# A pipelined two-layer window-attention and scan kernel: first loads moved ahead of the Toeplitz transfers, and own step tables for the first and the last rounds

## Chip, cores and metric

The kernel runs on one core of a Trainium2 chip. The metric is the device time of one execution in microseconds (us); the median of several runs is compared.

## The reference, cut to what matters

The input x has 32 images of 56 x 56 pixels with 96 channels. Two layers follow each other, each with a mixer and a feed-forward part, both added to their input.

```
x = x + attention(ln(x))     # 7x7 windows, 3 heads, rolled by 3 rows and columns
x = x + ffn0(ln(x))          # 96 -> 384 -> 96, fp8 products, fp16 sums, relu
x = x + scan(ln(x))          # expand and gate 96 -> 192, a linear recurrence along the
                             # 56 columns, times sigmoid(gate), 192 -> 96
x = x + ffn1(ln(x))          # as ffn0, with other weights
```

Within a row of 56 columns the recurrence is linear with fixed coefficients, so it is a product with a lower triangular Toeplitz matrix of 56 x 56 for each of the 192 channels. The kernel computes the 56 taps of each channel once, and then these matrices.

## The kernel before, in words

**Tiles.** An image is cut into 4 blocks of 14 rows, 128 blocks in all (`nblocks`). A block is one tile `xb` of 112 partitions by 7 by 96 floats, from a pool of 11 buffers; it is loaded in 6 DMAs (9 for the last block of an image, whose rows wrap round), worked on in place, and stored in as many. All loads and stores are issued by SyncE (SP), line 500 and line 506.

**Steps.** The work on a block is cut into 104 named steps, mostly one engine each. A name is a kind and a place. `s`, `p`, `n`, `t` are the four parts of a layer norm (`layer_norm`): statistics on VectorE (L442, L444), the power -1/2 on GpSimd (L450), the normalisation in seven instructions on VectorE (L460), the transpose on TensorE (L473, L475); the letter behind says which norm: `a` attention, `f` first feed-forward, `e` scan, `g` second feed-forward. `ea`, `ef`, `eg`, `xe` copy the transposed tile out of PSUM on ScalarE. Attention has `q`, `k`, `v`, `sc` (scores, L568), `st0` to `st2` (scores plus bias on VectorE, L599), `ex0` to `ex2` (exponential on ScalarE, L612), `av` (L650), `rc`, `tro`, `eo`, `pr` (L698), `ad` (add to xb, L492). A feed-forward part has `h`, `x`, `r`, `c` for three thirds (TensorE L718, ScalarE L730, VectorE L736, and the cast to fp8 at L742, on GpSimd for the second third and VectorE for the others), then `y` (TensorE L752), `z` (ScalarE L764), `b` (VectorE L770), `k` (GpSimd, add to xb, L774); so `hg2` is the first product of the third third of the second one. The scan has `r0` (GpSimd L795), `pu0` to `pu3` (L806, L807), `th` and `uc` (ScalarE L814, L819), and once in four blocks `SC0` to `SC5` (the Toeplitz products, L830) and `GA0` to `GA5` (gating on VectorE, L845); then `gt0`, `gt1` (transposes, L863), `eg0`, `eg1` (ScalarE L873), `so` (L884) and `as` (add to xb, L492). `LD` and `ST` are load and store.

**PSUM.** `banks` hands out four buffers of two banks each, in turn, to all steps that write PSUM; a step waits until the buffer of four steps earlier has been read.

**Order.** A table, `PIPELINED`, lists the steps as `name:lag`. The program is written out in rounds t = 0, 1, 2, ...; in a round each step of the table is issued, in the table's order, for block t - lag, if there is such a block. Lags go from 0 (`LD`) to 11 (`ST`, `zg`, `bg`, `kg`). So in the first rounds only the steps of small lag have a block, and in the last ones only those of large lag. Before the rounds are through, `add_manual_dep` fixes the order on each engine as written. Each engine works through its instructions in this order, and SP through its DMAs. A second table, `IN_TURN`, is for weights outside a bound; its branch isn't taken here.

**Toeplitz matrices.** VectorE makes the taps during the set-up. `load_toep`, called at the start of round 1, writes them repeatedly to a DRAM tile `taps_d` (one DMA of 4.7 MB, L266) and reads that back at skewed addresses in 18 DMAs (L274) into the two `gts` buffers, which later hold gates. `turn_toep`, at the start of round 5 (the smallest lag of a `th` step, since `th` is the first to write gates), copies them with two dimensions exchanged into `toep`, two copies on VectorE and two on ScalarE (L287).

Of the kernel before, what the change touches and what calls it, by code (L numbers as in the profile page):

```python
# [55 lines left out]
PIPELINED = (  # L56
# [7 lines left out]
)  # L64

IN_TURN = (
# [10 lines left out]
def kernel(  # L77
# [29 lines left out]
    nblocks = nimg * NBLK  # L107
# [32 lines left out]
    def zeros(size, name):  # L140
# [20 lines left out]
        fill=1.0,  # L161
# [71 lines left out]
    n = 1  # L233
# [29 lines left out]
    def load_toep():  # L263


        nc.sync.dma_start(taps_d.rearrange("w j e -> j w e"), taps_t[:, None, :].to_broadcast([2 * HW, HW, E]))  # L266
        src = taps_d[:, :, :]
        for half in (0, RS):

            for w0, w1 in ((0, 48), (48, HW - SH), (HW - SH, HW)):  # L270
                for t0, t1 in ((0, NRP), (NRP, HW - SH), (HW - SH, HW)):
                    w_in, w_out = (w0 + SH) % HW, (t0 + SH) % HW
                    first = w_in * 2 * HW + HW - w_in + w_out
                    nc.sync.dma_start(  # L274
                        gts[t0 // NRP][half + w0 : half + w1, t0 % NRP : t0 % NRP + t1 - t0].rearrange("w t e -> w (t e)"),
                        bass.AP(
                            tensor=src.tensor,
                            offset=src.offset + first * E,
                            ap=[[(2 * HW - 1) * E, w1 - w0], [1, (t1 - t0) * E]],
                        ),  # L280
                    )

    def turn_toep():
        toep3 = toep[:, 0 : E * HW].rearrange("p (e t) -> p e t", t=HW)
        for e0 in range(0, E, EH):
            for n, copy in enumerate((nc.vector.tensor_copy, nc.scalar.copy)):
                copy(  # L287
                    toep3[:, e0 : e0 + EH, n * NRP : (n + 1) * NRP],
                    gts[n][:, :, e0 : e0 + EH].rearrange("p t e -> p e t"),
                )  # L290
# [47 lines left out]
    def fill_bias(one):  # L338
        for b in bias:
            nc.vector.tensor_copy(b, one[:, None, :].to_broadcast([128, NPAIR, W2]))  # L340
        part = bias[1][:, NPAIR // 2 :, :]
        nc.vector.tensor_tensor(part, part, mask[:, None, :].to_broadcast([128, NPAIR // 2, W2]), ALU.add)
# [44 lines left out]
    for n in range(2):  # L387
# [10 lines left out]
        v = const.tile([128, NPAIR * NH, HD + 1], F32, name=f"v_{n}")  # L398
# [16 lines left out]
    step = {}  # L415
# [473 lines left out]
    feed_forward("g", 1)  # L889


    def pipeline(table):
        entries = [(n, int(lag)) for n, lag in (e.split(":") for e in table.split())]
        gates = min(lag for n, lag in entries if n[0:2] == "th")
        for t in range(nblocks + 1 + max(lag for _, lag in entries)):
            if t == min(1, gates):
                load_toep()
            if t == gates:
                turn_toep()
            for name, lag in entries:  # L900
                i = t - lag
                if name[0:2] in ("SC", "GA"):
                    if i % NBLK == 0 and 0 <= i < nblocks:
                        step[name](i // NBLK)
                elif 0 <= i < nblocks:
                    step[name](i)
        order = mybir.DependencyInfo(mybir.DependencyClass.NoSync, mybir.DependencyReason.DATA)
        last = {}
        for ins in nc.cur_bb.bb.instructions:
            if ins.engine in last:  # L910
                tc.add_manual_dep(ins, last[ins.engine], order, reason="order of the steps")
            last[ins.engine] = ins.name

    safe = nc.values_load(flag[0:1, 0:1], min_val=0, max_val=1)
    with tc.If(safe > 0) as branch:
        fill_bias(b1T)
        pipeline(PIPELINED)
    with branch.Else():
        fill_bias(b1)
        pipeline(IN_TURN)  # L920
# [49 lines left out]
```

## Time and profile before

| | |
|---|---|
| median of 3 runs | 3900.87 us (3891.35 to 3901.78) |
| the profiled execution | 3897.57 us, its span 3895.8 us |
| TensorE matmul busy | 3710.0 us, 95% of the span |
| VectorE busy | 3246.4 us, 83% |
| ScalarE busy | 2330.3 us, 60% |
| GpSimd busy | 1453.0 us, 37% |
| mean granted TensorE clock | 0.982 |
| bytes moved by DMA | 99.34 MB, 25 GB/s over the span |

The profile is one execution; its stretches are measured in microseconds from the start of the span. Busy time of TensorE (PE) counts matmuls, and PEld the loads of weights beside them. The granted clock is the share of TensorE's full clock that it was allowed in a stretch; the same matmul takes longer at a lower one. In the view of waits, a line names the waiting engine and line, what ended the wait, the total, how many times, and the longest.

Where the rounds stand in the span: the scores of block 0 (round 2) end at 44.24, the product `av` of block 0 (round 3) starts at 92.88, that of block 1 (round 4) at 113.56, the first copy of `turn_toep` (round 5) at 135.92, the first step of round 6 on TensorE at about 166.6 and of round 7 at 186.6. Round 130 starts at about 3737.6.

### The profile page before, as it was taken

The numbers are of one execution on the slowest core, as the hardware profiler recorded it, in microseconds if no ns is written. First come the engines' busy times: TensorE is split into PE (matmuls) and PEld (weight loads), VectorE is DVE, ScalarE is ACT, GpSimd is POOL, SyncE is SP. The second block draws the span as 40 slices with busy tenths as digits, with TensorE's granted clock in tenths as the row PEclk, the third lists the DMA queues.
The fourth block names the chain that finished last, engine by engine and source line by source line (L and its number), as shares of the span: only waits on it lengthen the run. The fifth ranks groups of instructions, "written<-read, shape, count | busy, mean of one in ns | idle before, by whom it ended". The sixth has DMA issues, their size and how long they took to land.

```text
span 3895.8 us, 178068 instructions
## 1 busy us (share of the span) xinstructions
PE 3710.0 (95%) x78628; PEld 3132.4 (80%) x78628; DVE 3246.4 (83%) x9420; ACT 2330.3 (60%) x4611; POOL 1453.0 (37%) x1176
## 2 busy tenths in 40 slices
PE   1899999999999999999999999999999999999996
PEld 1678888888888888888888888888888888888884
DVE  3678888888888888888888888888888888888864
ACT  0556666666666666666665666666666666656652
POOL 1333334333334343334433334433333433333432
PEclk7899999999999999999999999999999999999997
DMA  6000101001101011001110011110010100100100
GB/s 128 19 3 22 28 22 28 22 22 25 25 22 28 22 25 25 22 22 28 23 26 22 22 24 25 25 25 22 22 28 22 28 22 22 27 22 22 24 15 21
DMA packets 226267, 99.34 MB, mean 25 GB/s; under 512 B 218396, under 2 KB 225150, under 8 KB 225262
## 3 DMA queue, kind: packets, MB, share of 16 engines
q1 hardware_dynamic: 222522, 86.81, 9.9%
q8 instruction: 620, 10.16, 1.1%
q10 hardware_dynamic: 2964, 1.05, 0.1%
q14 instruction: 161, 1.32, 0.1%
HBM read 44.45 MB, written 43.35 MB: 23 GB/s over the span
## 4 chain that ended last, share of the span: by engine, by line
PE 89%; DVE 6%; DMA 2%; issue 1%; ACT 0%; POOL 0%; SPq 0%; ACTq 0%; DVEq 0%; POOLq 0%
PE pu L806 12%; PE scan L830 10%; PE so L884 9%; PE qk L526 7%; PE av L650 5%; PE gt L863 5%; PE pv L545 5%; PE pr L698 5%; PE pu L807 4%; PE s L568 4%; DVE pT L599 4%; PE py_g L752 4%; PE ph_g L718 4%; PE py_f L752 4%; PE tr_o L679 3%; PE ph_f L718 3%
## 5 line engine op out<-in xcount | busy, mean ns | idle before, releaser
L806 PE MATMUL pu<-weg,xs 128*128 128x288 f32 x1792 | 622.4, 429 | 0.7 <-issue 0.7
L730 ACT CAST h_g<-ph_g 128x784 f16<-128x784 f32 x384 | 300.3, 821 | 348.0 <-issue 330.4
L460 DVE TENSOR_SCALAR xn_g<-xb,st_g,rs_g 112x96 fp8e5<-112x96 f32 x896 | 365.8, 476 | 88.7 <-POOL rs_g L450 87.7
L830 PEld LDWEIGHTS scan<-u,toep 64*64 64x64 f32 x24576 | 386.4, 135 | 65.2 <-issue 42.9
L830 PE MATMUL scan<-u,toep 64*64 64x28 f32 x24576 | 413.8, 221 | 20.3 <-issue 18.9
L807 PEld LDWEIGHTS pu<-weg,xs 128*128 128x128 f32 x1792 | 341.4, 191 | 97.7 <-POOL xs L795 1.8
L819 ACT COPY u<-pu 128x384 f32<-128x384 f32 (+1 forms) x512 | 229.4, 448 | 298.3 <-PE pu L807 240.0
L742 POOL CAST hq_g<-h_g 128x784 fp8e5<-128x784 f16 x128 | 122.9, 960 | 751.6 <-DVE h_g L736 474.0
L450 POOL TENSOR_TENSOR rs_a<-rs_a,neg_half 112x7 f32<-112x7 f32 x128 | 190.8, 1490 | 560.1 <-DVE rs_a L444 560.1
L884 PEld LDWEIGHTS so<-wso,gT 128*112 128x112 f32 x3584 | 371.7, 179 | 9.1 <-PE ph_g L718 0.7
L884 PE MATMUL so<-wso,gT 128*112 128x96 f32 x3584 | 376.4, 263 | 0.0
L814 ACT ACTIVATE gt<-pu 128x384 f32<-128x384 f32 (+1 forms) x512 | 237.9, 465 | 212.2 <-PE pu L807 212.2
L845 DVE SCALAR_TENSOR_TENSOR gt<-gt,scan 128x448 f32<-128x448 f32 x384 | 220.5, 616 | 153.0 <-PE scan L830 152.9
L807 PE MATMUL pu<-weg,xs 128*128 128x96 f32 x1792 | 322.3, 262 | 2.6 <-issue 2.6
L526 PE MATMUL qk<-xw,wqkv 128*32 128x196 f32 (+1 forms) x3072 | 310.1, 394 | 2.6 <-ACT xw L516 2.3
L730 ACT CAST h_f<-ph_f 128x784 f16<-128x784 f32 x384 | 309.8, 807 | 1.7 <-DVE hq_g L742 0.9
L774 POOL TENSOR_TENSOR xb<-xb,y_f 112x672 f32<-112x672 f32 x128 | 187.3, 1463 | 292.4 <-DVE y_f L770 292.4
L806 PEld LDWEIGHTS pu<-weg,xs 128*128 128x128 f32 x1792 | 277.6, 192 | 18.9 <-issue 3.5
L650 PE MATMUL av<-v,pT 64*64 64x33 f32 x12288 | 212.7, 223 | 61.5 <-ACT pT L612 59.1
L718 PEld LDWEIGHTS <-w1q 128*128 128x128 fp8e5 x1536 | 123.0, 100 | 173.1 <-issue 79.2
L650 PEld LDWEIGHTS av<-v,pT 64*64 64x64 f32 x12288 | 196.9, 136 | 75.0 <-ACT pT L612 59.8
L599 DVE SCALAR_TENSOR_TENSOR pT<-s,bias 128x392 f32<-128x392 f32 (+1 forms) x512 | 213.6, 459 | 49.6 <-PE s L568 45.2
(147 smaller groups left out, 8653.0 us busy)
## 6 DMA issues: line engine op xcount, KB each, us to landing
xb<-in_x_dram SPq DMA_DIRECT2D x224, 126.0 KB
out_dram<-xb SPq DMA_DIRECT2D x224, 126.0 KB
taps_d<-u SPq DMA_DIRECT2D x1, 4704.0 KB
xb<-in_x_dram SPq DMA_DIRECT2D x224, 13.1 KB
xb<-in_x_dram SPq DMA_DIRECT2D x224, 7.9 KB
out_dram<-xb SPq DMA_DIRECT2D x224, 13.1 KB
out_dram<-xb SPq DMA_DIRECT2D x224, 7.9 KB
xb<-in_x_dram SPq DMA_DIRECT2D x32, 72.0 KB
```

What stands on the lines that cost most here:

```text
L460: nc.vector.tensor_scalar(xn[:, g, :], xb[:, g, :], mean[:, col], rs[:, col], op0=ALU.subtract, op1=ALU.mult, **saturate)
L526: nc.tensor.matmul(pq[j * rows : (j + 1) * rows, m, 0:size], wqkv[:, m * C + h0 * HD : m * C + h1 * HD], xws[i % 2][:, j * size : (j + 1) ...
L599: nc.vector.scalar_tensor_tensor(view(dst), src, QSCALE, view(bt), op0=ALU.mult, op1=ALU.add)
L650: nc.tensor.matmul(po[r * 64 : r * 64 + 64, k, n0 : n0 + HD + 1], pT[kp, h, pair * W2 : pair * W2 + 64], v[kp, pair * NH + h, :], start=Tr ...
L718: nc.tensor.matmul(ph[:, half, 0:HALF], w1q[:, hc * 128 : (hc + 1) * 128], xqs[layer][:, half * HALF : (half + 1) * HALF], start=True, sto ...
L730: nc.scalar.copy(h16.rearrange("p (h t) -> p h t", h=2), held.pop(("ph", n, i, hc))[:, :, 0:HALF])
L752: nc.tensor.matmul(po[:, g - g0, :], hq[hc][:, g * TP : (g + 1) * TP], w2q[:, hc, :], start=(hc == 0), stop=(hc == 2),)
L806: nc.tensor.matmul(pu[:, g, 0 : E + EH], rows[:, 0:128], weg[:, 0 : E + EH], start=True, stop=True)
L807: nc.tensor.matmul(pu[:, g, E + EH : 2 * E], rows[:, RS:], weg[:, E + EH :], start=True, stop=True)
L814: nc.scalar.activation(gt[:, rp : rp + n, :], held["pu", i, j][:, 0:n, 0:E], AF.Tanh, scale=0.5)
L830: nc.tensor.matmul(py[o0 : o0 + RS, eh, e * NRP : (e + 1) * NRP], toep[p * RS : (p + 1) * RS, ch * HW : ch * HW + RS], u[p * RS : (p + 1) ...
L884: nc.tensor.matmul(po[:, g - g0, :], gT[:, g - g0, eh, :], wso[:, eh, :], start=(eh == 0), stop=(eh == 1))
```

## The change

Three things are changed in `pipeline`, and two tables are added.

1. The loads of blocks 0 to 3 (`PRELOADED = 4`) are issued ahead of all rounds, and `load_toep` straight behind them, also ahead of the rounds. In the rounds `LD` issues only blocks from 4 on. `turn_toep` stays at the start of round 5.
2. Rounds 0 to 6 (`FILL_ROUNDS = 7`) follow a table `FILL`.
3. Rounds from 130 on (`nblocks + DRAIN_FROM`, 128 + 2) follow a table `DRAIN`. Rounds 7 to 129 follow `PIPELINED` as before.

Both tables hold the same 104 steps with the same lags as `PIPELINED`, in another order. In the branch of `IN_TURN` no other tables are given.

```diff
+FILL_ROUNDS = 7
+FILL = (
+    "gt0:9 hf0:4 r0:5 SC1:8 gt1:9 pu0:5 xf0:4 pg:10 ex2:3 hg1:10 SC2:8 ex0:3 pu1:5 eg:10 GA0:9 rf2:4 "
+    "cf1:4 pu2:5 xg1:10 th1:5 uc0:5 th2:5 SC5:9 rg1:10 ng:10 uc1:5 th0:5 ST:11 cg0:10 rg0:10 uc2:5 "
+    "cf2:4 sa:1 rf0:4 av:3 cf0:4 eg0:9 so:9 SC0:9 rc:3 kg:11 sg:9 GA2:9 zg:11 GA5:9 GA3:8 yf:4 zf:4 "
+    "tro:3 as:9 cg2:10 bf:4 kf:4 se:4 pa:1 ta:2 xg2:10 eo:3 GA1:8 rg2:10 ea:2 pe:4 pr:3 q:2 k:2 ad:3 "
+    "ek:2 bg:11 LD:0 yg:10 tg:10 pu3:5 uc3:5 cg1:10 sf:3 GA4:8 eq:2 th3:5 v:2 ne:4 ev:2 te:4 pf:3 "
+    "sc:2 xe:4 nf:3 tf:3 st1:2 ef:3 st0:2 st2:2 ex1:2 hf1:3 eg1:9 xf1:3 hg2:10 xg0:10 na:1 SC4:8 "
+    "hg0:10 hf2:3 xf2:3 SC3:8 rf1:3 "
+)
+DRAIN_FROM = 2
+DRAIN = (
+    "hf0:4 rf2:4 cf2:4 r0:5 SC5:9 xf0:4 LD:0 pu3:5 v:2 zg:11 pu2:5 uc3:5 eq:2 bg:11 st0:2 rf0:4 pg:10 "
+    "pu1:5 ex0:3 GA2:9 sa:1 cf1:4 th3:5 q:2 cf0:4 GA5:9 ng:10 th2:5 kg:11 ex2:3 uc2:5 yf:4 uc1:5 na:1 "
+    "SC0:9 GA0:9 st1:2 sc:2 th1:5 av:3 gt0:9 rc:3 zf:4 st2:2 bf:4 ea:2 tro:3 eo:3 eg0:9 ek:2 tg:10 "
+    "pr:3 pu0:5 eg:10 ad:3 gt1:9 hg2:10 sf:3 uc0:5 kf:4 se:4 eg1:9 pf:3 xg2:10 th0:5 SC4:8 nf:3 "
+    "hg0:10 tf:3 hg1:10 ta:2 rg2:10 xg1:10 pe:4 cg2:10 SC3:8 rg1:10 ef:3 pa:1 ne:4 xg0:10 GA4:8 "
+    "cg1:10 GA3:8 rg0:10 so:9 cg0:10 as:9 ev:2 hf1:3 hf2:3 SC2:8 ST:11 ex1:2 te:4 xf2:3 yg:10 xf1:3 "
+    "SC1:8 xe:4 GA1:8 sg:9 rf1:3 k:2 "
 )
...
-    def pipeline(table):
-        entries = [(n, int(lag)) for n, lag in (e.split(":") for e in table.split())]
-        gates = min(lag for n, lag in entries if n[0:2] == "th")
-        for t in range(nblocks + 1 + max(lag for _, lag in entries)):
-            if t == min(1, gates):
-                load_toep()
+    PRELOADED = 4
+
+    def pipeline(table, fill=None, drain=None):
+        tables = []
+        for text in (fill or table, table, drain or table):
+            tables.append([(n, int(lag)) for n, lag in (e.split(":") for e in text.split())])
+        gates = min(lag for n, lag in tables[0] if n[0:2] == "th")
+        for i in range(min(PRELOADED, nblocks)):
+            step["LD"](i)
+        load_toep()
+        for t in range(nblocks + 1 + max(lag for _, lag in tables[0])):
             if t == gates:
                 turn_toep()
-            for name, lag in entries:
+            for name, lag in tables[0 if t < FILL_ROUNDS else 2 if t >= nblocks + DRAIN_FROM else 1]:
                 i = t - lag
                 if name[0:2] in ("SC", "GA"):
                     if i % NBLK == 0 and 0 <= i < nblocks:
                         step[name](i // NBLK)
+                elif name == "LD":
+                    if PRELOADED <= i < nblocks:
+                        step[name](i)
                 elif 0 <= i < nblocks:
                     step[name](i)
...
-        pipeline(PIPELINED)
+        pipeline(PIPELINED, FILL, DRAIN)
```

More of the change, by code (lines that the diff above doesn't have):

```diff
@@ L63 @@
     "yg:10 sg:9 na:1 LD:0 rf1:3 "
+)
+FILL_ROUNDS = 7
+FILL = (
[7 rows of a table added]
+)
+DRAIN_FROM = 2
+DRAIN = (
[7 rows of a table added]
 )
```

## The prediction

> **What bounds the kernel now.** I read the 40 slices first, then busy time by stretch, the waits, and the chain of waits at both ends.
>
> ```profile
> span 3895.8 us, 178068 instructions
> ...
> PE   1899999999999999999999999999999999999996
> ...
> PEclk7899999999999999999999999999999999999997
> ```
>
> TensorE is at nine tenths in all slices but the first two and the last. Between the two ends it is the bound, and reordering the ends can't touch that. So I cut each end at its rounds (columns: stretch, length, busy us and instructions of PE, PEld, DVE, ACT, POOL, then granted clock, DMA share, GB/s).
>
> ```profile
> 89.30:113.56 24.26, 17.25 (x290) 12.99 (x290) 14.25 (x48) 9.15 (x18) 4.44 (x3) 0.70 0.47 108
> 113.56:135.92 22.36, 21.21 (x323) 17.29 (x324) 16.37 (x52) 8.58 (x17) 7.37 (x6) 0.69 0.01 2
> 135.92:166.60 30.68, 21.50 (x338) 17.51 (x337) 18.26 (x45) 20.62 (x27) 11.75 (x5) 0.78 0.01 2
> 166.60:186.60 20.00, 19.79 (x346) 15.41 (x347) 16.23 (x51) 12.94 (x28) 7.31 (x6) 1.00 0.01 2
> ```
>
> These are the end of round 2 with round 3, then rounds 4, 5 and 6. Round 6 is full (19.79 of 20.00). Round 5 is long because the turn of the Toeplitz matrices holds ScalarE for two copies (136.51 to 146.1). Before all that stands a hole, which the waits and the chain explain:
>
> ```profile
> DVE st_a L442 <- DMA xb<-in_x_dram: 55.4, 1, 55.4
> ```
>
> ```profile
> SPq L274 <- DMA gt<-taps_d: 28.1, 8, 7.1
> SPq L274 <- DMA taps_d<-u: 18.5, 1, 18.5
> SPq L266 <- DVE u L256: 10.7, 1, 10.7
> ```
>
> ```profile
> 22.97 18.87 DMA taps_d<-u
> ...
> 44.71 24.50 DMA gt<-taps_d
> 69.23 16.96 DMA gt<-taps_d
> 86.21 2.81 DMA xb<-in_x_dram
> ```
>
> VectorE waits once, for 55.4 us, for block 1. Its six loads stand on SP's queue behind the write of taps_d (from 22.97) and 18 reads of it; SP stops for each wait, so the loads are only issued from 78.64 to 86.2, and land at 89.0. Nothing else is missing then: the scores of block 0 ended at 44.24.
>
> The drain, by rounds 130, 131, 132, 133, 134, 135, 136, and 137 with the end:
>
> ```profile
> 3737.60:3760.60 23.00, 21.18 (x264) 17.83 (x264) 18.11 (x56) 15.88 (x33) 10.43 (x9) 0.97 0.06 15
> 3760.60:3780.10 19.50, 17.18 (x134) 14.20 (x133) 13.41 (x36) 10.57 (x21) 9.26 (x8) 0.85 0.07 16
> 3780.10:3799.30 19.20, 18.74 (x471) 16.44 (x472) 7.30 (x17) 7.62 (x16) 2.29 (x2) 0.92 0.08 18
> 3799.30:3826.70 27.40, 20.23 (x481) 17.11 (x481) 15.28 (x36) 6.31 (x10) 4.89 (x4) 0.81 0.06 14
> 3826.70:3841.70 15.00, 10.23 (x81) 8.01 (x80) 8.40 (x22) 5.50 (x9) 3.88 (x3) 0.87 0.10 22
> 3841.70:3857.40 15.70, 12.12 (x81) 9.69 (x79) 8.00 (x20) 5.50 (x9) 3.95 (x3) 0.69 0.08 19
> 3857.40:3874.40 17.00, 10.45 (x80) 8.07 (x77) 9.18 (x24) 6.28 (x11) 5.59 (x5) 0.83 0.09 19
> 3874.40:3895.80 21.40, 6.65 (x34) 3.94 (x34) 6.04 (x13) 3.89 (x7) 3.60 (x3) 0.50 0.15 33
> ```
>
> No engine is full from round 133 on: a chain from engine to engine sets the length, and part of PE's busy time is a halved clock (so takes 3.9 us at a low clock and 2.9 at a full one).
>
> [...] the 24 qk matmuls took 4.35 us at 36.7 and 2.34 us at 124.4 (the record of the granted clock says full speed in both[...]). [...] here xn_g takes 2.90 us for seven beside the xb add of GpSimd and 1.77 without it, in the drain too, and no order given by the tables parts them.
>
> **Part 1, loads in front.** Nothing is removed or added: 27 DMAs of blocks 0 to 3 (6, 6, 6 and 9) are issued before the taps_d write; 21 of them move past 19 transfers. Block 0's six took 2.42 us from 9.73 (0.40 each), so all end at 9.73 + 27 x 0.40 = 20.6. SP sat idle there anyway, in the 10.7 us that it waits for VectorE's taps, to 22.97. So the Toeplitz transfers start as before; the cover is 2.3 us wide, and if loads run slower, the excess delays the turn one for one. Their 1.2 MB should have landed by about 24 (2.8 us after the last issue, as at 86.2). I take 0 to 3 us of delay, value 0.5. Block 4's load now stands where block 1's did and lands at 89; it is first wanted in round 5 after the turn, so it costs nothing.
>
> Without the hole: sa of block 1 runs at 34 beside PE's work, and the score sums (st, 90.57 before) start when the scores end, at 44.35. From 90.57 to the turn's first copy (135.92) is 45.35 us, so with the old order the turn is reached at 44.35 + 45.35 = 89.7. The turn waits for the reads too. The last large one ended at 86.2; the small ones behind it I put at 87.5 (86.2 to 89). Behind the waiting turn stand, on VectorE, rf2, cf1 and sa of block 4, on ScalarE xf0 and ex2, and for these waits PE with av of block 2, once hf0 and three pu are through. So arrival and transfers come within 2 us of each other: **the stall that goes is succeeded at once by the Toeplitz transfers**, and no order of rounds 2 to 4 brings more than 135.9 - 86.2 = 49.7.
>
> **Part 2, the table for rounds 0 to 6.** Each step keeps its lag, so only the order on the engines changes. In rounds 3 and 4 sc comes before nf and tf, and the sums st follow nf, not sc: in round 4 before, VectorE ended xn_e at 131.76 and st began at 132.08, then xn_a and the turn; some 1.7 us of it overlap now. Against it, xf0 (0.81) stands before ex2 and ex0. Arrival 87 to 90; with the transfers' 87.5 + 0.5 the turn begins at about 88.5, so **47.4 us** come out (43 to 50). Round 5: pu2 now runs while ScalarE turns (1.4 us at full clock, 2.7 as at 149.7), xf0 costs 0.8 behind it: 1 us gained. The change of order at round 7 may cost as much (0 to 2, unseen in the trace). Fill: **47 us**, 42 to 52. From round 7 to 129 the order is the same and PE is full, so the shift stays.
>
> **Part 3, the table from round 130.** Rounds 134 to 136: the path runs as - cg0, rg1, rg2, cg2 - st_g - rs_g - xn_g - tr_g - gt1 - ph_g - so - as. Between as and st_g lie 0.47 + 0.68 + 1.09 = 2.24 us of VectorE casts; the new order puts sg straight behind as, and the casts beside so. In return hg2 (0.5) goes ahead of so, and xg0, rg0, cg0 end 0.3 after so does at best[...]. Net 2.2 a round by three rounds: 6.6. The last block has the same casts taken out before its st_g and none of the losses count in full: 2.2. Round 132/133: from so of block 123 (ends 3796.9) to that of 124 (3822.5) are 25.6 us, with 4.5 us of PE standing still between scans and about 2 of low clock; PE's work in it at full clock is 15.5, VectorE's chain (as, GA1, sg, GA2, GA5, ng, GA0) some 10 and gt, eg, so behind it 7. I take 19.6: 6.0. Round 131: before, ne (1.77) stands ahead of as, both h_g steps and cg2, and py_g waits for these until 3778; rg2, cg2 and rg1 now go ahead of it: 3. Round 130 has only 2 us in which PE isn't busy: 1. Sum 18.8; the change of order at 130 I charge 0.8 (0 to 3). **Drain 18 us**; low end 4 (only the casts, and half of them), high end 26.
>
> Behind the last add (ends 3887.9) nine stores and their landing take 8 us as before.
>
> **Sum.** 47 + 18 = 65. The profiled execution took 3897.57 (span 3895.8): 3832.6. The median of the three runs is 3.3 above it, so I take 3834 for a median.
>
> **Rivals.** (a) The forecast, 3834: 0.60. (b) The drain stays bound by the same chain, since its casts only move to stand ahead of as: fill 47, drain 4: 3850 (0.17). For it: py_g and xg0 need those casts in every round; against it: so takes 2.8 us or more, in which VectorE idles 2.1 to 3.2 us now. (c) The transfers take over in the fill: loads and reads collide, or the reads run slower beside a working core; turn at 95, fill 40, drain 16: 3845 (0.10). Against it: the loads fit into SP's idle time. (d) More in both, 52 + 26: 3823 (0.08). (e) **Slower**: an order handed over at round 7 with loads and stores at another phase makes each of the 123 steady rounds longer (28.87 us each: 186.6 to 3737.6). Saving is gone at 65 / 123 = 0.53 us a round, and it is slower by 0.3% at 0.62; at 0.75 it gives 3927. Against it: after 89 us no load was waited for again (one wait of 55.4 in all). 0.03. That the loads don't go ahead at all is excluded by block 0's, issued in its written place at 9.73; with the tables alone it would be near 3880 (0.02, with the same).
>
> **Range.** What a measurement can tell from no change here is about 0.3%, 12 us. (a), (b) and (c) reach from fill 52 and drain 26 to fill 42 and drain 4, with some 4 us between runs: 3815 to 3857. Left out are (e), the tables alone and half of (d). Faster 0.95, same 0.02, slower 0.03.
>
> **What would show it.** No st_a wait over 5 us; 27 xb loads on SP before 22.97; the turn's first copy at 87 to 90, released by gt or just behind it; PE busy from 45 to 88 with gaps in place of a hole; first hf0 of round 6 near 118; st_g straight behind as from round 133; so to so about 13 us in rounds 134 to 136. I am wrong if taps_d starts after 26, if a wait for gt holds the turn past 93, or if rounds 10 to 129 differ by more than 0.05 us each.

## The result, and the profile after

| | before | changed |
|---|---|---|
| median, four runs each on one chip | 3896.11 us (3883.43 to 3901.78) | 3844.48 us (3839.45 to 3848.43) |
| ratio, 95% interval | | 0.9871 (0.9842 to 0.9901) |
| the profiled execution, and its span | 3897.57, 3895.8 us | 3844.57, 3842.8 us |

51.6 us came out of the medians, where 65 were forecast; a second measurement of the pair (e9 below) gave 43.6. The time lies inside the range. The sum behind it does not hold in three of its terms: the start of the turn, round 130, and the step from `so` of block 123 to that of block 124.

The page of the changed kernel, the lines that answer to those of before:

```profile
span 3842.8 us, 178057 instructions
...
PE   4899999999999999999999999999999999999996
...
PEclk8999999999999999999999999999999999999997
```

The hole in the first slices is smaller (4 and 8 for 1 and 8), not gone. Three boundaries that can be found in both traces split the profiled difference of 53.0 us: `av` of block 7, the start of `so` of block 119, and the end.

| stretch | before | changed | difference |
|---|---|---|---|
| start to `av` of block 7 | 268.3 | 227.5 | -40.8 |
| to `so` of block 119, steady rounds | 3425.5 | 3418.8 | -6.7 |
| to the end | 202.1 | 196.5 | -5.6 |

**The steady rounds are noise here.** Their order is unchanged, and in twelve other profiles with the same order there they took 3419.5 to 3436.7, in a second one of the changed kernel 3428.5. So the change itself shows as 46 us in this pair.

**The fill.** SyncE's queue, by its timeline (start, duration, instruction, how many) and by its waits:

```profile
9.73 10.69 SPq L521 DMA_DIRECT2D xb<-in_x_dram  x27
23.29 0.32 SPq L287 DMA_DIRECT2D taps_d<-u  x1
42.27 35.03 SPq L295 DMA_DIRECT2D gt<-taps_d  x18
```

```profile
SPq L295 <- DMA gt<-taps_d: 28.2, 8, 7.4
SPq L295 <- DMA taps_d<-u: 18.6, 1, 18.6
...
SPq L287 <- DVE u L277: 2.8, 1, 2.8
```

The 27 loads fit into the idle time, as costed: the wait for VectorE's taps shrank from 10.7 to 2.8, and taps_d starts 0.3 later. The wait of 55.4 us for block 1 is gone. Yet the turn starts at 95.17, not at 88.5, and it waits for nothing: ScalarE works up to it (its timeline).

```profile
93.76 1.53 ACT L751 CAST h_f<-ph_f 128x784 f16<-128x784 f32 x2
95.17 9.55 ACT L308 COPY toep<-gt 128x2688 f32<-128x2688 f32 x2
```

So it is the arrival that is late. The chain of work shows where:

```profile
58.06 2.47 issue
...
63.59 7.90 issue
```

"issue" is time in which the engine waited for nothing that the profile shows. TensorE's timeline puts both stops inside a step (in brackets the idle time ahead):

```profile
55.73 2.33 PE L547 MATMUL qk<-xw,wqkv 128*64 128x392 f32 x23
60.53 0.33 PE L547 MATMUL qk<-xw,wqkv 128*32 128x196 f32 x1 [2.47 <-issue]
...
62.26 1.32 PE L589 MATMUL s<-qk 32*64 32x49 f32 x95
71.49 0.34 PE L589 MATMUL s<-qk 32*64 32x49 f32 x1 [7.90 <-issue]
```

The 24th matmul of `qk` and the 96th of `s` have the same inputs and the same bank as their neighbours, so the program has nothing that these two alone would wait for. Together the stops are 10.37 us, and the other engines run dry: in the second one, by busy time in stretches, VectorE, ScalarE and GpSimd did nothing, with the DMA engines full (share 1.05).

```profile
63.60:71.50 7.90, 0.01 (x1) 0.01 (x1) 0.00 (x0) 0.00 (x0) 0.00 (x0) 0.62 1.05 154
```

**The drain.** The chain behind one `so` of the last rounds, first before (`so` of block 124), then in the changed kernel (`so` of block 125):

```profile
3822.52 0.92 DVE xb L492 x2
...
3824.62 1.08 DVE hq_g L742
3825.70 1.07 DVE st_g L442 x4
```

```profile
3785.22 3.22 PE so L905 x28
...
3788.46 0.92 DVE xb L513 x2
3789.38 1.07 DVE st_g L463 x4
```

`st_g` now follows the add `as` at once; the 2.24 us of casts are out of the path. In rounds 134 to 136 the steps from `so` to `so` are 12.9, 13.8 and 13.8 us, for 15.8, 14.8 and 15.9 before. But round 130 is longer than before (below).

### The profile page after: what moved, and what is told of

It reads as the page before. It is cut to its first block, busy times and chain, and to the rows that moved or that the text cites. A ratio compares the mean times of both kernels' runs of the same rounds, so it can differ in the third digit from the quotient of the medians.

```text
span 3842.8 us, 178057 instructions
## 1 busy us (share of the span) xinstructions
PE 3695.3 (96%) x78628; PEld 3124.7 (81%) x78628; DVE 3247.2 (84%) x9420; ACT 2329.9 (61%) x4611; POOL 1452.0 (38%) x1176
## 3 DMA queue, kind: packets, MB, share of 16 engines
q8 instruction: 620, 10.16, 1.1%
q10 hardware_dynamic: 2964, 1.05, 0.1%
q14 instruction: 161, 1.32, 0.1%
## 4 chain that ended last, share of the span: by engine, by line
PE 91%; DVE 6%; issue 2%; ACT 1%; POOL 0%; DMA 0%; SPq 0%; DVEq 0%; ACTq 0%; POOLq 0%
PE pu L827 13%; PE scan L851 10%; PE so L905 9%; PE qk L547 8%; PE av L671 5%; PE gt L884 5%; PE pv L566 5%; PE pr L719 5%; PE pu L828 4%; PE s L589 4%; DVE pT L620 4%; PE ph_g L739 4%; PE py_g L773 4%; PE py_f L773 4%; PE tr_o L700 3%; PE ph_f L739 3%
## 5 line engine op out<-in xcount | busy, mean ns | idle before, releaser
L481 DVE TENSOR_SCALAR xn_g<-xb,st_g,rs_g 112x96 fp8e5<-112x96 f32 x896 | 365.0, 476 | 95.1 <-POOL rs_g L471 94.4
L840 ACT COPY u<-pu 128x384 f32<-128x384 f32 (+1 forms) x512 | 229.1, 448 | 291.4 <-PE pu L828 235.3
L894 ACT COPY gT<-gt 96x896 f32<-96x896 f32 (+1 forms) x256 | 209.4, 818 | 76.4 <-PE gt L884 73.5
L481 DVE TENSOR_SCALAR xn_f<-xb,st_f,rs_f 112x96 fp8e5<-112x96 f32 x896 | 226.2, 326 | 33.4 <-POOL rs_f L471 33.4
```

Source lines behind the costliest of these rows:

```text
L481: nc.vector.tensor_scalar(xn[:, g, :], xb[:, g, :], mean[:, col], rs[:, col], op0=ALU.subtract, op1=ALU.mult, **saturate)
L840: nc.scalar.copy(u[:, rp : rp + n, :], held["pu", i, j][:, 0:n, E : 2 * E])
```

## Experiments

Theory **A**, for the stops: TensorE's own instructions come late, since they come by DMA beside the long packets of the Toeplitz reads. Rival **B**: the stops come from the new order of the rounds. Two readings make A possible. The pages of both kernels list a DMA queue of instructions with 620 packets and 10.16 MB, 16 KB each:

```profile
q8 instruction: 620, 10.16, 1.1%
```

TensorE has 78,628 matmuls and as many weight loads (page of before), which makes 254 instructions for each packet, if the queue is TensorE's alone. And in the changed kernel 1 + 32 + 95 = 128 matmuls lie between the two stops, each with its weight load, 256 instructions.

**One part at a time: e1 (loads only), e2 (loads and fill table), e3 (drain table only).**

```diff
 # e1
-        pipeline(PIPELINED, FILL, DRAIN)
+        pipeline(PIPELINED)
 # e2
+        pipeline(PIPELINED, FILL)
 # e3: and load_toep back at the start of round 1
-    PRELOADED = 4
+    PRELOADED = 0
+        pipeline(PIPELINED, None, DRAIN)
```

> Loads of four blocks in front, the old table in all rounds. Theory A (TensorE's instructions come late behind the long reads of the Toeplitz transfers): TensorE stands still in the middle of a step for some 10 us in all between 45 and 88 us, the turn's first copy at 96 to 100, round 6 some 37 to 41 us earlier than before, time 37 to 41 us below before. Theory B (the stalls come from the new table's order): no such stall, the turn at 88 to 91, time about 46 us below before.

> Loads in front and the table for rounds 0 to 6; the old table in the drain. If the drain's table is worth 6 us (the new round 130 gives back what the later rounds win): 4 to 8 us above the changed kernel, so from round 120's so to the end 199 us as before. If it is worth the 18 us of the prediction: 18 us above it.

> Only the table for the drain; loads and first rounds as before. Drain worth 6 us: 4 to 8 us below before, from so of block 119 to the end 193 us in place of 199. Drain worth 18 us: 15 to 20 below before.

| | median us | ratio to before | turn | `av` of block 7 | `so` 119 to end |
|---|---|---|---|---|---|
| e1 | 3864.88 | 0.9910 (0.9887 to 0.9933) | 95.2 | 229.1 | 205.0 |
| e2 | 3857.5 | 0.9886 (0.9861 to 0.9911) | 95.2 | 224.9 | 202.2 |
| e3 | 3889.14 | 0.9978 (0.9967 to 0.9989) | 132.7 | 265.7 | 198.0 |

The loads bring 33.7 us of medians, the fill table 7.4 more (4.2 at block 7 in the profiles), the drain table 9.4. The parts add up: 41.1 and 9.4 for 51.6. The part of the fill table isn't clear of the noise: the intervals of e1 and e2 overlap, and six profiles with this fill reach block 7 at 224.9 to 230.4 (e1: 229.1). The drain table alone, with twenty runs, is worth 4 to 13 us (the interval of e3), so the 18 of the prediction are ruled out. On the other expectations: e1's saving of 33.7 us is below the 37 to 41 of A, and far from the 46 of B; e2 ends 5.7 us later after `so` of block 119 than the changed kernel, in the branch of a small drain. B falls with e1: in the old order TensorE stops as well, again 128 matmuls apart (32 + 7 + 89), now ahead of `pv` and inside `s`:

```profile
60.33 1.54 PE L566 MATMUL pv<-wqkv,xw 128*64 128x96 f32 x32 [1.59 <-issue]
61.80 0.55 PE L494 MATMUL tr_f<-ident,xn_f 112*96 112x112 fp8e5 x7
62.28 1.25 PE L589 MATMUL s<-qk 32*64 32x49 f32 x89
71.19 0.46 PE L589 MATMUL s<-qk 32*64 32x49 f32 x7 [7.66 <-issue]
```

**The long reads away: e4 (changed kernel), e10 (the same with the old order throughout).**

```diff
                 for t0, t1 in ((0, NRP), (NRP, HW - SH), (HW - SH, HW)):
+                    if t1 - t0 > SH:
+                        continue
```

> The changed kernel without the Toeplitz reads that have more than 3 rows of taps in one run (4.4 of 4.6 MB), so that the scan's matrices aren't those of the reference. Theory A: no stall of TensorE over 1 us in the middle of a step between 45 and 88 us, the turn's first copy at 84 to 88 (only the order of steps decides), time 7 to 11 us below the changed kernel. Theory B: the two stalls of 2.5 and 7.9 us stay, the turn at 95, time as the changed kernel.

> Loads in front, the old table in all rounds, and no Toeplitz reads of more than 3 rows of taps (the scan's matrices aren't those of the reference). Arrival at the turn by the old order alone: 89.7 by the prediction's sum; if TensorE at a full clock shortens rounds 3 and 4 whatever the order, 84 to 87. The new table reaches it at 83.4, so the difference is what the table is worth there.

Both leave out most of the Toeplitz reads, so they serve for timing alone. e4: 3838.66 us, ratio 0.9839 (0.9815 to 0.9862); turn at 83.45, `av` of block 7 at 215.0. The median is 5.8 us below the changed kernel's, for 7 to 11 expected, and the intervals overlap; it is the trace that decides. The same 24 and 96 matmuls of TensorE's timeline now run through:

```profile
54.95 2.34 PE L549 MATMUL qk<-xw,wqkv 128*64 128x392 f32 x24
...
58.69 1.34 PE L591 MATMUL s<-qk 32*64 32x49 f32 x96
```

e10 (one run, 3857.06) reaches the turn at 86.2 and block 7 at 219.5. So without stops and without waiting for the transfers the old order arrives at 86.2 and `FILL` at 83.45; the table is worth 2.7 us at the turn and 4.5 at block 7, by one profile each.

**The same bytes in shorter packets: e5 (rows of 7 instead of 28), e5b (fewer rows in one DMA, packets as long as before).**

```diff
 # e5
-                for t0, t1 in ((0, NRP), (NRP, HW - SH), (HW - SH, HW)):
+                for t0, t1 in ((0, 7), (7, 14), (14, 21), (21, 28), (28, 35), (35, 42), (42, 49), (49, 53), (53, 56)):
 # e5b
-            for w0, w1 in ((0, 48), (48, HW - SH), (HW - SH, HW)):
+            for w0, w1 in ((0, 16), (16, 32), (32, 48), (48, HW - SH), (HW - SH, HW)):
```

> The changed kernel with each Toeplitz read cut along the taps into reads of at most 7 rows of taps: 54 reads, packets of at most 5.4 KB in place of 21.5, the same bytes. If long packets hold up TensorE's instructions, or the bytes of the eight reads in flight do (8 of 258 KB in place of 8 of 1 MB): stalls of TensorE between 45 and 88 us fall from 10.4 to under 3 us, the turn starts when the reads have landed, 86 to 89, time 6 to 9 us below the changed kernel. If only the total of bytes counts: stalls as before, turn at 95.

> The changed kernel with the reads of 48 partitions cut into three of 16: 30 reads, packets as long as before (21.5 KB), but a third of the bytes in each read in flight. If the length of a packet holds up the instructions: stalls stay near 10 us, turn near 95. If the bytes queued ahead do: stalls under 4 us, turn at 86 to 90.

In e5 the stops shrink from 10.37 to 1.67 us, at the same two matmuls:

```profile
58.30 0.33 PE L547 MATMUL qk<-xw,wqkv 128*32 128x196 f32 x1 [0.89 <-issue]
...
62.13 0.25 PE L589 MATMUL s<-qk 32*64 32x49 f32 x1 [0.78 <-issue]
```

VectorE's first copy now starts at 87.9 and does wait for the reads, as it did not in the changed kernel (waits in 80 to 98 us):

```profile
ACT toep L308 <- DMA xb<-in_x_dram: 3.8, 1, 3.8
...
DVE toep L308 <- DMA gt<-taps_d: 1.7, 1, 1.7
```

ScalarE's starts at 89.65; the name of its releaser is that of the last DMA event before it. In e5b, with the long packets, TensorE stops for 4.60 and 2.74, 7.3 us together, and the turn is at 95.1, after VectorE has waited 1.1 us and ScalarE 2.8 us for a DMA. In the other five kernels with long packets and this fill (e2, e6, e7, e9, e11) the two stops add up to 9.2 to 12.2 us, in e8 below, with short ones, to 2.2.

In blocks of 256, the distance of the stops, the 620 packets of queue 8 hold 158,720 instructions, and TensorE's are 157,256; by this count, an estimate, the queue is TensorE's. The packet list of the traces shows when two of them came, beside it when TensorE went on by its timeline:

| | read packets of 19.2 and 21.5 KB, mean of each | first block: start, took, end | TensorE on | second block: start, took, end | TensorE on |
|---|---|---|---|---|---|
| changed | 2.1 and 2.3 us | 56.83, 1.71, 58.54 | 60.53 | 68.34, 1.67, 70.01 | 71.49 |
| e1 | the same | 56.70, 1.63, 58.33 | 60.33 | 67.83, 1.75, 69.58 | 71.19 |
| e5b | as long, 2.65 and 2.55 us | 58.85, 1.92, 60.77 | 62.18 | 65.78, 1.78, 67.56 | 69.34 |
| e5 | 5.4 KB in their place, 0.53 us | 54.79, 1.55, 56.34 | 58.30 | 59.41, 1.28, 60.69 | 62.13 |
| e4 | none over 3 rows | 47.36, 1.51, 48.87 | no stop | 56.04, 1.32, 57.36 | no stop |

In eight stops of four kernels TensorE goes on 1.4 to 2.0 us after a block of 256 instructions has come. Against e4 the first of the two blocks came 9.5 to 11.9 us later with the long packets and 7.5 with the short ones, the second 10.2 to 12.7 and 3.3. That is A: the stops are late instructions. How late they came followed the length of the read packets. SyncE had eight reads under way before it waited for the first (in the changed kernel issued from 42.27 to 46.03, the ninth at 52.53); by their sizes these hold 2.3 MB in the changed kernel (not 8 MB, as the expectation of e5 has it), 1.9 in e5 and 2.0 in e5b. So the bytes in line differ little, e5b has more and smaller DMAs, as e5 has, and only the length of a packet is as before; with it most of the stops stay. The short packets didn't remove all: the first block of e5 still comes 7.5 us later than in e4, with a stop of 0.89. Not shown is the queueing itself; no record says where in line an instruction packet stood.

On the clock e5 (3853.52 us, 0.9884, 0.9853 to 0.9916) and e5b (3851.0, 0.9875, 0.9845 to 0.9905) can't be told from the changed kernel: the 6 us of e5 at block 7 (221.4 for 227.5; e5b 226.5) are within the spread of the steady rounds. The 6 to 9 us expected of e5 are seen at block 7 alone.

**The drain: e6 (table from round 131), e7 (from 132), e11 (the old order from round 130 with `sg` alone put straight behind `as`).**

```diff
 # e6: 3, e7: 4
-DRAIN_FROM = 2
+DRAIN_FROM = 3
 # e11
-        pipeline(PIPELINED, FILL, DRAIN)
+        pipeline(PIPELINED, FILL, PIPELINED.replace("sg:9 ", "").replace("as:9 ", "as:9 sg:9 "))
```

> The changed kernel with the drain's table from round 131 on, round 130 in the old order. If the new order makes round 130 itself longer (so of block 120 to so of block 121 28.8 us in place of 22.6): that step is 22.6 again, the later ones keep most of their gain, from so of block 119 to the end 188 to 192 us in place of 196.5, time 4 to 8 us below. If only the change from one order to the other costs, wherever it stands: the 6 us move to round 131 and the time stays within 2 us.

> The changed kernel with the drain's table from round 132 on. If the new order suits rounds 132 to 138 alone: from so of block 119 to the end 190 to 194 us (round 131's 2 us of gain are lost, round 130's 6 us of loss too). If a change of order costs 6 us wherever it stands: 198 us or more.

> The changed kernel with another drain table: the old order with one step moved, sg straight behind as. If the casts between as and sg are what round 134 to 136 wait for (2.24 us a round): so to so falls from about 15.5 to 13.3 there, round 130 stays at 22.6, from so of block 119 to the end about 193. If the casts only move the wait to py_g: so to so stays above 15.

Steps from one `so` to the next, means over the profiles of four kernels with the old drain (before, e1, e2, e10) and six with `DRAIN` from round 130 (changed, e3, e4, e5, e5b, e9 below):

| | 119-120 | 120-121 | 121-122 | 122-123 | 123-124 | 124-127 | to the end | sum |
|---|---|---|---|---|---|---|---|---|
| old | 34.9 | 22.6 | 20.8 | 23.3 | 24.7 | 46.4 | 31.0 | 203.7 |
| `DRAIN` | 35.0 | 28.9 | 17.7 | 19.1 | 24.3 | 40.4 | 29.7 | 195.1 |
| e6 | 35.0 | 22.6 | 20.4 | 19.1 | 24.5 | 40.5 | 29.7 | 191.9 |
| e7 | 35.3 | 22.6 | 18.5 | 22.4 | 24.1 | 39.7 | 29.4 | 192.3 |

`so` of block 121 is in round 130, and with `DRAIN` it comes 6.3 us later. With the table from round 131 on (e6: 3847.75 us, 0.9862, 0.9833 to 0.9892) or from 132 (e7: 3848.53, 0.9867, 0.9837 to 0.9896) this step is as before. But half of the 6.3 us is only work that now stands ahead of `so` and no longer behind it: the next step is 17.7 us with `DRAIN` and 20.4 in e6, so that the two steps together are 46.6 us with `DRAIN`, 43.4 in the old order and 43.1 in e6. Round 130 thus costs some 3.5 us. The end comes 191.9 and 192.3 after `so` of block 119 in e6 and e7, and 191.3 in e8 below; with `DRAIN` from round 130 it is 192.6 to 198.0 in six profiles, 195.1 in the mean. The times can't tell e6 and e7 from the changed kernel: the 4 to 8 us expected of e6 are not seen there. Why, in TensorE's timeline of the changed kernel in round 130:

```profile
3696.11 1.28 PE L773 MATMUL py_f<-w2q,hq_f 128*112 128x96 fp8e5 x21 [1.30 <-DVE hq_f L763]
3697.32 1.60 PE L671 MATMUL av<-v,pT 64*64 64x33 f32 x96
...
3708.34 1.69 PE L494 MATMUL tr_f<-ident,xn_f 112*96 112x112 fp8e5 x7 [1.48 <-DVE xn_f L481]
...
3710.20 4.51 PE L905 MATMUL so<-wso,gT 128*112 128x96 f32 x28
```

Block 127 is in round 130 with its whole middle, from `av` to `tf`. In `DRAIN` its `av` stands behind `py_f` of block 126, which waits for its casts, and `so` behind block 127's `tf`; TensorE stands still for 1.30, 0.53, 0.65 and 1.48 us ahead of `so`, together 4.0: that is what is lost. It also runs `tr_f` for 1.69 first, which is only moved. e6 in the old order starts `av` between the `pu` products and has `tr_f` behind `so`:

```profile
3705.87 1.60 PE L671 MATMUL av<-v,pT 64*64 64x33 f32 x96
...
3715.95 2.90 PE L905 MATMUL so<-wso,gT 128*112 128x96 f32 x28
...
3719.02 0.51 PE L494 MATMUL tr_f<-ident,xn_f 112*96 112x112 fp8e5 x7
```

The step from `so` of block 123 to that of block 124, for which the prediction booked 6.0, hardly moved in any kernel (23.1 to 25.9 us in all fourteen profiles). The prediction counted 4.5 us in which TensorE stood still there. In TensorE's timeline of before, 3.65 of these are stops of the same kind as in the fill:

```profile
3799.97 2.05 PE L830 MATMUL scan<-u,toep 64*64 64x28 f32 x123 [0.43 <-issue]
...
3803.45 0.98 PE L752 MATMUL py_g<-w2q,hq_g 128*112 128x96 fp8e5 x16 [0.82 <-issue]
...
3807.19 2.07 PE L830 MATMUL scan<-u,toep 64*64 64x28 f32 x128 [1.00 <-issue]
3810.66 0.65 PE L830 MATMUL scan<-u,toep 64*64 64x28 f32 x16 [1.40 <-issue]
```

They lie 128 matmuls apart (123 + 5, 16 + 112, 128), and each ends 1.3 to 1.5 us after a 16 KB packet has come on queue 8. No long reads run there (DMA share 0.06): 128 of these small matmuls take 2.07 us, and the packets come 3.5 to 3.6 us apart. The changed kernel has them again, 3.3 us in all (its chain):

```profile
3752.83 0.26 issue
...
3755.87 1.24 issue
...
3759.39 1.55 issue
...
3764.58 0.21 issue
```

So the new order did not remove them. That they alone set the length of the step isn't shown: in other profiles the stops are shorter there (e1: 0.8 us) and the granted clock lower (0.70 for 0.84), with about the same length (25.2 for 24.6).

e11 (one run, 3866.04 us) came out on the second branch of its expectation: the last steps stay above 15, at 16.7, 16.7 and 16.6 us, and are even longer than the 15.8, 14.8 and 15.9 of before. Its chain says why:

```profile
3817.90 0.92 DVE xb L513 x2
3818.82 1.06 DVE st_g L463 x4
...
3820.08 0.47 DVE hq_g L763
3820.55 0.68 DVE h_g L757 x2
...
3821.25 1.09 DVE hq_g L763
...
3822.39 1.99 PE py_g L773 x19
...
3825.34 0.51 DVE y_g L791
3825.85 1.63 DVE xn_g L481 x2
```

The casts were only moved behind the statistics. There they delay `py_g`, whose bias add (L791) stands ahead of `ng` on VectorE. The place of `sg` alone is worth nothing. `DRAIN` also takes `hg2` and the casts ahead of `as`, beside `so`; that this is what makes it pay is likely, but no run changes it alone.

**Both repairs, e8 (e5 and e6 together), beside the changed kernel once more, e9.**

> The changed kernel with both repairs: the reads cut to 7 rows of taps, and the drain's table from round 131. If both stages add up: the turn at 88, av of block 7 at 221, from so of block 119 to the end 192 us, so 6 + 3 = 9 us below the changed kernel of the same call (within the spread of some 5 us between runs). If the stages between give it back: no difference beyond 3 us.

> The changed kernel again, as the measure for the one before. Turn at 95, stalls of TensorE of some 10 us between 56 and 72, from so of block 119 to the end 193 to 197 us; 46 to 55 us below before.

e8: 3847.92 us (3842.45 to 3859.01, five runs), ratio 0.9867 (0.9847 to 0.9888), turn at 88.5, block 7 at 221.7, the end 191.3 after `so` 119, as expected. e9: 3860.0 (3850.06 to 3864.41, six runs), 0.9886 (0.9868 to 0.9905), turn at 95.1, block 7 at 227.0, the end 195.5; it is 43.6 us below before, a little less than the 46 to 55 expected. The two ends together are 9.6 us shorter in e8; the medians differ by 12, but the two intervals still overlap. So e8 is probably the better kernel, and these runs don't prove it.

## Why the forecast was right, and where it was not

- **27 loads in SyncE's idle time: right.** They end at 20.42 (20.6 forecast) and delay taps_d by 0.3 (0.5).
- **Arrival at the turn: a little pessimistic.** 89.7 forecast for the old order, 86.2 in e10; 87 to 90 for `FILL`, 83.45 in e4.
- **The Toeplitz transfers as next in line: right as a bound, overtaken by another.** e5 shows it: with the stops nearly gone the copies start at 87.9 and 89.65, for the 88.5 forecast.
- **The turn at 88.5: the step that failed.** It was at 95.2. The sum took the reads and TensorE's work as independent up to the turn. The runs showed 10.4 us of stops in TensorE by late instructions; the path has 84.8 + 10.4 in place of 88.5. Their size couldn't be read from the trace of before, since TensorE stood idle from 44 to 89 (no packet came on queue 8 from 41.2 to 94.0) and had no instructions to miss; that such stops exist could, in round 133. Rival (c) named the size, turn at 95 and fill 40, but with the direction reversed: it let the working core slow the reads, and the reads slowed the core. That its sum, 3845, was met is chance: its drain of 16 was not.
- **Fill 47: 40.8** in this pair. To the turn 40.7 (47.4 forecast), from there to `av` of block 4 2.3 (1 forecast), and from block 4 to block 7 2.2 lost (0 to 2 for the change of order at round 7).
- **No change in rounds 7 to 129: right**, within what the steady rounds scatter by themselves. No later wait for a load replaced the saving, so rival (e) falls.
- **Drain 18: 8.5** over ten profiles, 5.6 in this pair. Rounds 134 to 136 gave 6.0 of 6.6, where the net of 2.2 a round was an estimate, the end 1.3 of 2.2. `so` itself was no shorter there: 2.96, 4.04 and 3.00 us before, 3.41, 3.34 and 3.27 in the changed kernel. Round 131 was booked at 3 and gave 4.2 in the step to `so` of block 123; e7, which keeps the old order there, has only 0.9 of it.
- **The step from `so` of block 123 to that of 124: failed.** It was booked at 6.0 and gave 0.4. The prediction took TensorE's standing still there for waits that an order can close; 3.65 of the 4.5 us were late instructions, and 3.3 us of them remained.
- **Round 130: failed.** It was booked as a gain of 1 against 0.8 for the change of order, and cost some 3.3 us against the old order (46.6 for 43.4 us in its two steps). Busy shares alone hid this: TensorE was full there in the old order (busy for 21.18 of 23.00 us), and the new one opened gaps of 4.0 us.
- **Rival (b), a drain of 4 as casts only move: not the case** in rounds 134 to 136, where its mechanism would act, though e11 shows that the mechanism exists. Its size is nearer to the 8.5 than the forecast is, for another reason.

For the profiled execution the sum was 3832.6, and it took 3844.57: of these 12.0 us, 6.2 are of the fill and 12.4 of the drain, less the 6.7 by which its steady rounds happened to be shorter.

## What to carry to other kernels

When a wait is removed early in a kernel, the engines start working in a stretch that was idle before. Here TensorE's instructions came 9.5 to 12.7 us later in that stretch beside the long reads than without them, so look at which long DMA packets run there, and try shorter ones: in e5 they took the stops from 10.4 to 1.7 us, though no gain of the whole kernel is proven. When an engine stands still in the middle of a step for "issue", count its instructions from one stop to the next (here 256) before booking the time as a gain. In round 130, which was already full, the new order lost; a table of its own is better begun at the first round that has gaps. A step moved ahead, as in e11, is worth nothing if what it passes is then late for the next engine.

## What the runs showed of the hardware

**Late instructions.** Beside read packets of 19.2 and 21.5 KB (2.1 and 2.3 us each) the instruction packets of 16 KB came so late that TensorE stopped for 10.4 us in two places 256 instructions apart; with packets of 5.4 KB (0.53 us) for 1.7, without the reads for none. In round 133 of before, with a DMA share of 0.06, it stopped four times for 0.4 to 1.4 us, where 128 small matmuls took 2.07 us and the instruction packets came 3.5 to 3.6 us apart.

**Dips of the clock.** In steady rounds that were full, the granted clock fell to one half for 3.4 to 20.5 us, one to three times in each of the other twelve profiles, often near places that two to four of them share. In e2, for one (columns as in the stretches above):

```profile
1237.90:1258.40 20.50, 20.50 (x390) 17.62 (x389) 8.13 (x21) 4.38 (x10) 4.56 (x4) 0.50 0.04 9
```

TensorE was busy all the time, and VectorE for 8.13 us; in the same stretch of the changed kernel, at a granted clock of 1.00, VectorE was busy for 16.85. The same matmuls took longer at a lower clock: the 28 of `so` in the drain of before 2.99 us at 1.00 and 4.04 at 0.70. The profiles of the first pair have no such dip in the steady rounds; others do, and the spread is 18 us for the same instructions in the same order (3418.8 to 3436.7). 17 of the 21 dips begin within 1.2 us after TensorE has stood still for 0.8 to 1.7 us with "issue" (in e2 for 1.01 us, to 1236.93). But the steady rounds of the fourteen profiles have 122 such stops (9 and 8 in the first pair, with no dip), so what sets a dip off stays open.
